# Four convolution layers on one core: the weights' preparation reordered, the interval layer's right products on two row tiles, roots by Newton steps, and fewer transfers for the images' parts

## The chip, the cores and the metric

One core of one Trainium2 chip runs the whole program. The metric is the device time of one execution in microseconds (us); it is compared as a median over several executions.

## What is computed

The input `x` is 4 images of 32 x 32 pixels with 16 channels, all fp32. Four layers follow, each with a group norm before it and a residual sum around it:

```python
x = x + conv(_gn(x), L0_M, L0_W, L0_G)
x = x + conv(_gn(x), L1_M, L1_W, L1_G)
x = x + interval(_gn(x), W0, b0, W1, b1, W2, b2)
x = x + conv(_gn(x), L3_M, L3_Wp, L3_G)
```

`_gn` subtracts a mean and divides by `sqrt(var + 1e-5)`, over all pixels and pairs of channels. In `conv`, each of the 1024 output positions has a 3 x 3 kernel of its own, from 16 to 16 channels:

```python
first   = einsum('ijyx,byxc->bijc', M, inputs)
shifted = conv2d(inputs, kernels of all (i, j, f))       # b, i, j, y, x, f
diff    = relu(inputs[:, None, None] - shifted)
second  = einsum('ijyx,bijyxc->bijc', W, diff)
return first - second
```

The interval layer takes running maxima and minima over a 32 x 32 table of each channel, and then two steps of `max_k sigmoid(f[i, k] Wf + r[k, j] Wr + b)` and a last product with a sigmoid.

## The kernel before

The images are worked on in two groups of two (`g` = 0, 1). A **phase** is one group in one of the three convolution layers; there are six, in the order (0,0), (1,0), (0,1), (1,1), (0,2), (1,2) of (group, layer). A phase has 8 chunks of 128 output positions, a chunk 32 **steps**, one for each of 16 channels `f` and 2 images `b`. So the program has 1536 steps, numbered here from 0. A step makes a 128 x 1024 sum in one of four pairs of PSUM banks: output positions on partitions, input pixels along the row, the left half of the image in one bank and the right half in the other.

**A step.** `first_part` (L642) issues eight fp32r matmuls with `ib` and `ia`, then ScalarE scales the sum in place (L663). `second_part` (L666), issued one step later, adds six matmuls with `iyz` and `im9`; then VectorE takes the minimum with zero, multiplies by the row of weights `WT` and sums (L680, output `junk`). Every product runs as two matmuls of 64 rows, on the upper and lower half of TensorE's rows. The 16 steps of the first two units (`u < PLAIN`) use plain fp32 products instead.

**Weights.** A unit `u` is four channels, eight steps; it is used in steps 8u to 8u + 7. `prep_parts` (L220) is a generator that is advanced once a step, from step `FIRST` = 3 on, and twice in steps 20 and 24. Its cycle has eight positions for each unit: the upper bits of the weights by VectorE (`upper`, L203); a masked copy `W9` by ScalarE (`halve`, L175); a scaled and a plain copy by ScalarE (L236, L240); differences, sums and four quarter copies by GpSimd (L237, L238, L241, L243, L245); `prep` of the next unit by GpSimd (L214); and at the seventh position two transfers on SyncE's queue that exchange halves of partitions of `parts` (L251), followed by the load of the raw weights of the unit after next (L110). Each `yield` names what other work may be done at that position: `IDLE`, `CALM`, both or none.

**Other work.** The generator `behind(phase)` (L733) prepares the next phase during this one and is advanced by `conv_layer` (L707) after the matmuls of a step have been issued. A positive number that it yields is a number of steps to wait; `IDLE` and `CALM` wait for a position of the weights' cycle that allows it. In it, `group_norm` (L312) makes mean and variance by VectorE and GpSimd and the root by ScalarE (L353, L358), with a reciprocal by VectorE (L360). `before_conv` (L368) transposes the normed images (L375), writes them to DRAM by eight transfers (`xs`, L381) and reads 24 shifted copies back (`raw`, L392), two a step, in layer 2 four a step. Then `split` (L274) takes upper and lower parts of an image (L203, L280, L284), `place` (L290) puts them into `ia` and `ib` by twelve transfers (L298, L300), `difference` (L286) makes `iyz` on GpSimd (L288), and `halve` and `halve_rest` (L178) make `im9`. `first_terms` (L418) makes the einsum with `M`: 128 matmuls on TensorE. `interval_layer` (L484) works on tables by VectorE scans (L527), GpSimd copies and selections (L534, L538) and products on TensorE: `left` (L544) and `right_side` (L555). The latter makes three blocks of 352, 231 and 110 columns one after the other, a step apart, each in a bank pair of its own, and ScalarE copies each to `rt` (L564).

**Order.** All is under `manual_schedule`: every engine and SyncE's queue works in the order in which the program issues, and waits in that order for what each instruction needs. Within a step the order is: the weights' generator, the first part, the second part of the step before, then `behind`.

Of the kernel before, what the change touches and what calls it, by code (L numbers as in the profile page):

```python
# [44 lines left out]
def net_kernel(ctx: ExitStack, tc: tile.TileContext, x, xq, xi, convs, iv_w, iv_b, out):  # L45
# [40 lines left out]
    def bank(name):  # L86
        return bank_pair(name)[:, 0]
# [131 lines left out]

    def prep_parts():  # L220
# [3 lines left out]

        for u in range(PLAIN, n_chunks * NU):
# [20 lines left out]
            yield ()  # L246
            prep(u + 1)
            yield (IDLE,)
            yield (IDLE, CALM)
            for h in range(2):  # L250
                nc.sync.dma_start(  # L251
                    parts[64 * h : 64 * h + 64, 1].bitcast(F32),
                    parts[64 - 64 * h : 128 - 64 * h, 0].bitcast(F32),
                )
            load_raw(u + RAWS)
            yield (IDLE, CALM)
            yield (IDLE, CALM)
# [12 lines left out]
    def halves(temp, b):  # L270
        v = temp.rearrange("p (k s b n) -> p k s b n", k=2, s=2, b=GB)
        return v[:, 0, :, b], v[:, 1, :, b]
# [17 lines left out]
    def place(g, b, temp):  # L290

        ty, tz = (v.bitcast(F32) for v in halves(temp, b))
        da, db = (v[g].bitcast(F32)[:, :, b] for v in (ia, ib))
        for h, (lo, hi) in enumerate(QUARTERS):
            for s in range(2):
                at = HW if s == h else 0
                for to, src in ((lo, ty), (hi, tz)):
                    nc.sync.dma_start(da[to, s, :LAST], src[lo, s, at : at + LAST])  # L298
            for to, src in ((lo, ty), (hi, tz)):
                nc.sync.dma_start(db[to], src[hi])  # L300
        yield 1
# [7 lines left out]
    def pair_view(ap):  # L309
        return ap.rearrange("p t (g s) -> p t g s", s=2)  # L310

    def group_norm(g, name, dst, gap):  # L312
# [55 lines left out]
    def before_conv(g, layer):  # L368
# [29 lines left out]
        temp = big.tile([P, 8192], F32R, tag="big", name=f"temp_{g}{layer}")[:, :TEMP]  # L398
# [19 lines left out]
    def first_terms(layer, mt):  # L418
# [3 lines left out]
        for g in range(NG):  # L422
            for pt in range(NT):
                for j in range(4):
# [4 lines left out]
                    )  # L429
        ft = work.tile([P, NG, NT * GC], F32, tag="fs", name=f"ft_{layer}")  # L430
# [15 lines left out]
    def constants():  # L446
# [7 lines left out]
        nc.gpsimd.tensor_scalar_mul(mask2[GC : 2 * GC], mask2[GC : 2 * GC], -1.0)  # L454
# [23 lines left out]
        for k, name in ((1, "r0"), (4, "r1")):  # L478
            t = const.tile([64, NQ * GB, C], F32, name=name)
# [4 lines left out]
    def interval_layer(g):  # L484
# [56 lines left out]
        )  # L541
        yield 5
# [12 lines left out]
        def right_side(name, wr):  # L555

            for k0 in range(0, T1, 11):
                j0 = k0 + 1
                ps = bank(f"ps_{name}{g}{k0}")
                n = T1 - j0  # L560
                nc.tensor.matmul(  # L561
                    ps[:, : 11 * n], lhsT=wr, rhs=r[:R, k0 : k0 + 11, j0:], start=True, stop=True
                )
                nc.scalar.copy(  # L564
                    rt[:, j0:, k0 : k0 + 11],
                    ps[:, : 11 * n].rearrange("p (k j) -> p j k", j=n),
                )
                yield 1
# [411 lines left out]
```

## Time and profile before

| what | us |
|---|---|
| median of three runs | 2478.37 (2478.10 to 2479.17) |
| the profiled execution | 2478.41 |
| its span, first to last instruction | 2476.7 |
| TensorE matmuls busy | 2458.2 |
| VectorE busy | 2087.3 |
| ScalarE busy | 1878.4 |
| GpSimd busy | 1579.7 |
| L680, VectorE, 1536 times | 1879.5 |
| L663, ScalarE, 1520 times | 1532.0 |
| five table loads on ScalarE, 1.283 each | 6.4 |
| landing of the exchange of halves, median | 4.9 |

The profile is of one execution; its own time of 2478.41 us has 1.7 us around the span. Busy shares are of the span. In lines of the timeline the first number is the start and the second the length, in us from the span's start; "x4" after the shape is the number of instructions merged into the line, and the bracket names what ended the idle time before it. `PE` is TensorE's matmuls, `PEld` its loads of stationary weights, `DVE` VectorE, `ACT` ScalarE, `POOL` GpSimd, and `SPq` the issuing of transfers by SyncE.

### The profile page before, as it was taken

Reading aid. Unit: us, or ns where it says so; the run is one execution under the profiler, and the core shown is the slowest. Engines: PE = TensorE matmul, PEld = TensorE weight load, DVE = VectorE, ACT = ScalarE, POOL = GpSimd, SP = SyncE. Lnnn points to the kernel's source line nnn. Section 1 sums busy time; section 2 is a strip of 40 time slices with the busy share of each in tenths; the row PEclk is TensorE's granted clock in tenths of the full one; section 3 lists DMA queues with packets and bytes.
Section 4 is the critical chain, followed back from the end, with each engine's and each line's share of the span. In section 5 each row is a group of like instructions: output and inputs, shape, how many; then the busy total and the mean of one; then the engine's idle time right before and its main releaser. Section 6 shows DMA issues by size and latency. Waiting matters only on the chain.

```text
span 2476.7 us, 58058 instructions
## 1 busy us (share of the span) xinstructions
PE 2458.2 (99%) x21906; PEld 2090.1 (84%) x21906; DVE 2087.3 (84%) x3617; ACT 1878.4 (76%) x2181; POOL 1579.7 (64%) x1750
## 2 busy tenths in 40 slices
PE   8999999999999999999999999999999999999999
PEld 5999888888888888888888988888998888888887
DVE  9888878888888888778898988899889888788887
ACT  4778767787777778777777777787777787677776
POOL 4766655666565657555567777586878676555552
PEclk9999999999999999999999999999999999999999
DMA  6446754466454467644454545574455467554442
GB/s 198 138 137 182 203 155 135 124 182 164 133 143 135 135 168 198 186 116 134 136 145 127 142 124 140 146 196 125 126 138 144 127 181 195 154 148 137 137 137 54
DMA packets 97673, 366.92 MB, mean 148 GB/s; under 512 B 26480, under 2 KB 31472, under 8 KB 97392
## 3 DMA queue, kind: packets, MB, share of 16 engines
q1 hardware_dynamic: 96832, 362.79, 53.0%
q8 instruction: 172, 2.82, 0.5%
q14 instruction: 109, 0.89, 0.1%
q10 hardware_dynamic: 432, 0.39, 0.1%
q0 software_dynamic: 128, 0.02, 0.0%
HBM read 199.78 MB, written 1.02 MB: 81 GB/s over the span
## 4 chain that ended last, share of the span: by engine, by line
PE 94%; DVE 2%; issue 1%; DMA 1%; ACT 0%; SPq 0%; POOL 0%; ACTq 0%; DVEq 0%; POOLq 0%
PE pc L627 93%; DVE junk L680 1%; PE pf L425 1%; DMA raw<-in_g 1%; ACT pc L663 0%; DMA first<-in_g 0%; SPq L298 0%; DVE raw L846 0%; SPq L300 0%; PE ps_l L548 0%; PE ps_r L561 0%; DMA parts<-parts 0%; DVE tables L508 0%; DVE raw L854 0%; DMA ib<-first 0%
## 5 line engine op out<-in xcount | busy, mean ns | idle before, releaser
L680 DVE SCALAR_TENSOR_TENSOR junk<-pc,WT 128x1024 f32<-128x1024 f32 x1536 | 1879.5, 1224 | 359.1 <-PE pc L627 308.3
L663 ACT ACTIVATE pc<-pc 128x1024 f32<-128x1024 f32 x1520 | 1532.0, 1008 | 561.0 <-PE pc L627 535.8
L627 PE MATMUL pc<-ib,parts 64*128 64x512 f32 x6080 | 958.5, 388 | 4.1 <-DVE junk L680 3.4
L627 PE MATMUL pc<-iyz,parts 64*128 64x512 f32 x6080 | 955.5, 387 | 2.2 <-ACT pc L663 2.0
L627 PE MATMUL pc<-ia,parts 64*128 64x496 f32 x6080 | 933.5, 379 | 0.0
L627 PEld LDWEIGHTS pc<-ia,parts 64*128 64x128 f32 x6080 | 595.5, 184 | 100.8
L627 PEld LDWEIGHTS pc<-ib,parts 64*128 64x128 f32 x6080 | 591.5, 184 | 105.0 <-DVE junk L680 9.9
L627 PEld LDWEIGHTS pc<-iyz,parts 64*128 64x128 f32 x6080 | 592.5, 184 | 88.4 <-ACT pc L663 6.4
L627 PE MATMUL pc<-im,W 64*128 64x496 f32 x3072 | 611.5, 384 | 0.0
L237 POOL TENSOR_TENSOR parts<-raw,upper_w 128x512 fp32r<-128x512 f32 x190 | 248.5, 1308 | 500.2 <-DVE upper_w L203 434.8
L627 PEld LDWEIGHTS pc<-im,W 64*128 64x128 f32 x3072 | 303.0, 184 | 54.5 <-issue 3.2
L243 POOL CAST parts<-parts 32x512 fp32r<-32x512 f32 x380 | 231.1, 608 | 50.1 <-ACT parts L240 31.8
L238 POOL TENSOR_TENSOR W<-W,raw 128x512 fp32r<-128x512 f32 x190 | 247.6, 1303 | 1.8 <-ACT W L175 1.8
L241 POOL TENSOR_TENSOR parts<-parts 128x512 fp32r<-128x512 f32 x190 | 246.8, 1299 | 2.0 <-ACT parts L236 1.9
L245 POOL CAST parts<-upper_w 32x512 fp32r<-32x512 f32 x380 | 231.6, 609 | 22.8
L214 POOL TENSOR_TENSOR raw<-raw,ident 128x512 f32<-128x512 f32 x190 | 199.9, 1052 | 52.2 <-DMA raw<-in_g 28.7
L175 ACT ACTIVATE W<-raw,low_w 128x512 fp32r<-128x512 f32 x190 | 136.2, 717 | 0.1
L680 DVE DVE_READ_ACCUMULATOR junk<-pc,WT 128x1 f32 x1536 | 127.5, 83 | 0.0
L236 ACT ACTIVATE parts<-upper_w 128x512 fp32r<-128x512 f32 x190 | 118.8, 625 | 6.6 <-DVE upper_w L203 6.4
L240 ACT CAST parts<-upper_w 128x512 fp32r<-128x512 f32 x190 | 116.5, 613 | 0.0
L695 POOL TENSOR_SCALAR acc<-acc 128x32 f32<-128x32 f32 x40 | 16.4, 409 | 141.7 <-DVE junk L680 139.7
L203 DVE TENSOR_SCALAR upper_w<-raw 128x512 int32<-128x512 int32 x190 | 86.1, 453 | 1.2 <-POOL raw L214 0.9
(139 smaller groups left out, 479.4 us busy)
## 6 DMA issues: line engine op xcount, KB each, us to landing
raw<-in_g SPq DMA_DIRECT2D x190, 768.0 KB, 7.1
parts<-parts SPq DMA_DIRECT2D x380, 384.0 KB, 4.9
WT<-in_w SPq DMA_DIRECT2D x48, 512.0 KB, 4.6
MT<-in_mt SPq DMA_DIRECT2D x24, 512.0 KB, 7.4
raw<-xs SPq DMA_DIRECT2D x120, 71.8 KB, 2.9
ib<-temp SPq DMA_DIRECT2D x40, 128.0 KB, 2.6
ia<-temp SPq DMA_DIRECT2D x80, 62.0 KB, 3.4
ib<-first SPq DMA_DIRECT2D x8, 128.0 KB, 2.4
```

What stands on the lines that cost most here:

```text
L175: nc.scalar.activation(dst, src, AF.Copy, scale=mask[:, 1:2])
L214: eng.tensor_tensor(raws[u][:, s, at:to], raws[u][:, s, at:to], pick[s][:, f0 + at : f0 + to].unsqueeze(2).to_broadcast([P, to - at, P]), ...
L236: nc.scalar.activation(WD, high, AF.Copy, scale=-EPS)
L237: nc.gpsimd.tensor_tensor(WL, w8, high, ALU.subtract)
L238: nc.gpsimd.tensor_tensor(W9, W9.bitcast(F32), src[:, 2], ALU.add)
L240: nc.scalar.copy(WU, high)
L241: nc.gpsimd.tensor_tensor(WD, WD.bitcast(F32), WL.bitcast(F32), ALU.add)
L243: nc.gpsimd.tensor_copy(WU[hi], WL[lo].bitcast(F32))
L245: nc.gpsimd.tensor_copy(WL[lo], high[hi])
L627: nc.tensor.matmul(ps[:, h, at : at + n], lhsT=w[r], rhs=v[r] if n == NH else v[r][:, :n], start=first and k == 0, stop=k == len(pairs) - ...
L663: nc.scalar.activation(ps, ps, AF.Copy, scale=1.0 + EPS)
L680: nc.vector.scalar_tensor_tensor(junk, ps.rearrange("p h n -> p (h n)"), 0.0, chunks[n], op0=ALU.min, op1=ALU.mult, accum_out=accs[phase][ ...
```

## The change

1. **The weights' cycle.** The masked copy `W9` comes first and the upper bits second, into a tile `high` of their own. The sum for `W9` and `prep` of the next unit come one operation group earlier, the quarter copies later, and the next load moves from the seventh position to the fifth. The exchange of halves moves to the second position of the next unit's cycle. The two extra advances are in steps 17 and 20.
2. **Right products.** The table `r` is copied to partitions 64 to 127 and the weights `r0`, `r1` are made for 128 partitions. The block of 352 columns runs on the first row tile, the blocks of 231 and 110 columns on the second, all issued together into one pair of banks. ScalarE's three copies are still a step apart.
3. **Roots.** The group norms' root and reciprocal are replaced by `inverse_root`: a start value from the bits of the number, by VectorE, and four Newton steps of four GpSimd operations each, spread over steps. The activation that loaded the Sqrt table ahead goes, and so does the one for the Sigmoid table in each interval step; a Sigmoid activation stands once in the first terms of layer 0.
4. **Images' parts.** `place` uses eight transfers instead of twelve: the four of `ib` first, then four of `ia`, each with two slots.
5. **Order of steps.** In the first chunk of each phase, not only of the first, the steps of each unit take image 0 first and then image 1.
6. `squares` uses the scratch tile `junk`, and `temp` is passed whole and cut in `halves`.

```diff
+    def exchange(parts):
+        if parts is not None:
+            for h in range(2):
+                nc.sync.dma_start(
+                    parts[64 * h : 64 * h + 64, 1].bitcast(F32),
+                    parts[64 - 64 * h : 128 - 64 * h, 0].bitcast(F32),
+                )
+
     def prep_parts():
+        swapped = None
         for u in range(PLAIN, n_chunks * NU):
...
-            high = upper(src[:, 0:1], 1, f"w{u}")[:, 0]
-            yield (IDLE,)
             halve(W9, src[:, 1], low_w)
             yield ()
+            high = work.tile([P, FU * P], F32, tag="high", bufs=2, name=f"high_{u}")
+            nc.vector.tensor_scalar(
+                high.bitcast(I32), w8.bitcast(I32), HIGH, None, op0=ALU.bitwise_and
+            )
+            exchange(swapped)
+            yield (IDLE,)
             nc.scalar.activation(WD, high, AF.Copy, scale=-EPS)
             nc.gpsimd.tensor_tensor(WL, w8, high, ALU.subtract)
-            nc.gpsimd.tensor_tensor(W9, W9.bitcast(F32), src[:, 2], ALU.add)
             yield ()
             nc.scalar.copy(WU, high)
+            nc.gpsimd.tensor_tensor(W9, W9.bitcast(F32), src[:, 2], ALU.add)
+            prep(u + 1)
+            yield ()
             nc.gpsimd.tensor_tensor(WD, WD.bitcast(F32), WL.bitcast(F32), ALU.add)
             for lo, hi in QUARTERS:
                 nc.gpsimd.tensor_copy(WU[hi], WL[lo].bitcast(F32))
             for lo, hi in QUARTERS:
                 nc.gpsimd.tensor_copy(WL[lo], high[hi])
-            yield ()
-            prep(u + 1)
+            load_raw(u + RAWS)
+            swapped = parts
             yield (IDLE,)
-            yield (IDLE, CALM)
-            for h in range(2):
-                nc.sync.dma_start(
-                    parts[64 * h : 64 * h + 64, 1].bitcast(F32),
-                    parts[64 - 64 * h : 128 - 64 * h, 0].bitcast(F32),
-                )
-            load_raw(u + RAWS)
-            yield (IDLE, CALM)
-            yield (IDLE, CALM)
+            for _ in range(3):
+                yield (IDLE, CALM)
+        yield (IDLE, CALM)
+        exchange(swapped)
...
     def place(g, b, temp):
...
+        for lo, hi in QUARTERS:
+            for to, src in zip((lo, hi), parts):
+                nc.sync.dma_start(db[to], src[hi])
         for h, (lo, hi) in enumerate(QUARTERS):
-            for s in range(2):
-                at = HW if s == h else 0
-                for to, src in ((lo, ty), (hi, tz)):
-                    nc.sync.dma_start(da[to, s, :LAST], src[lo, s, at : at + LAST])
-            for to, src in ((lo, ty), (hi, tz)):
-                nc.sync.dma_start(db[to], src[hi])
+            for k, to in enumerate((lo, hi)):
+                at = (2 * k * GB + b) * NH + HW * (1 - h)
+                pitch = GB * NH + HW * (2 * h - 1)
+                src = temp.bitcast(F32)[lo, at : at + 2 * pitch].rearrange("p (s n) -> p s n", s=2)
+                nc.sync.dma_start(da[to, :, :LAST], src[:, :, :LAST])
...
+    def inverse_root(v, name):
...
+        nc.gpsimd.tensor_scalar(a, v, 1.0 / (2 * NP), 1e-5, op0=ALU.mult, op1=ALU.add)
+        nc.vector.tensor_scalar(
+            t.bitcast(I32), a.bitcast(I32), 1, None, op0=ALU.logical_shift_right
+        )
+        nc.vector.tensor_scalar(
+            y.bitcast(I32), t.bitcast(I32), -1.0, float(0x5F3759DF), op0=ALU.mult, op1=ALU.add
+        )
+        nc.gpsimd.tensor_scalar_mul(a, a, -0.5)
+        for pause in (1, 1, IDLE, 2):
+            yield pause
+            nc.gpsimd.tensor_tensor(t, a, y, ALU.mult)
+            nc.gpsimd.tensor_tensor(t, t, y, ALU.mult)
+            nc.gpsimd.tensor_scalar(t, t, 1.5, None, op0=ALU.add)
+            nc.gpsimd.tensor_tensor(y, y, t, ALU.mult)
+        return y
...
-        nc.scalar.activation(spare, spare, AF.Sqrt)
         v = yield from totals(f"v{name}")
-        yield 2
-        yield IDLE
-        rstd = work.tile([P, GC // 2], F32, tag="rstd", name=f"rstd_{name}")
-        nc.scalar.activation(rstd, v, AF.Sqrt, bias=eps, scale=1.0 / (2 * NP))
-        yield 2
-        nc.vector.reciprocal(rstd, rstd)
+        rstd = yield from inverse_root(v, name)
...
+        if layer == 0:
+            nc.scalar.activation(spare, spare, AF.Sigmoid)
...
+        below = tables[R:, : T1 * T1].rearrange("p (i j) -> p i j", j=T1)
+        nc.gpsimd.tensor_copy(below, r[:R])
+        tops = (r[:R], below)
         yield 5
...
-            for k0 in range(0, T1, 11):
+            ps = bank_pair(f"ps_{name}{g}")
+            blocks = []
+            for k0, h, at in ((0, 0, 0), (11, 1, 0), (22, 1, 11 * (T1 - 12))):
                 j0 = k0 + 1
-                ps = bank(f"ps_{name}{g}{k0}")
                 n = T1 - j0
+                blocks.append((k0, j0, n, ps[:, h, at : at + 11 * n]))
                 nc.tensor.matmul(
-                    ps[:, : 11 * n], lhsT=wr, rhs=r[:R, k0 : k0 + 11, j0:], start=True, stop=True
+                    blocks[-1][3], lhsT=wr[R * h : R * h + R], rhs=tops[h][:, k0 : k0 + 11, j0:],
+                    start=True, stop=True,
                 )
+            for k0, j0, n, sums in blocks:
                 nc.scalar.copy(
...
-            nc.scalar.activation(spare, spare, AF.Sigmoid)
             yield 2
...
-            if n == 0:
+            if t == 0:
                 steps.sort(key=lambda s: (s[0] // FU, s[1]))
...
-                if n == 0 and at in (20, 24):
+                if n == 0 and at in (17, 20):
                     next(parts)
```

More of the change, by code (lines that the diff above doesn't have):

```diff
@@ L270, in halves @@
     def halves(temp, b):
-        v = temp.rearrange("p (k s b n) -> p k s b n", k=2, s=2, b=GB)
+        v = temp[:, :TEMP].rearrange("p (k s b n) -> p k s b n", k=2, s=2, b=GB)
         return v[:, 0, :, b], v[:, 1, :, b]
@@ L290, in place @@
     def place(g, b, temp):
-        ty, tz = (v.bitcast(F32) for v in halves(temp, b))
+        parts = halves(temp.bitcast(F32)[:, :TEMP], b)
         da, db = (v[g].bitcast(F32)[:, :, b] for v in (ia, ib))
+        for lo, hi in QUARTERS:
+            for to, src in zip((lo, hi), parts):
+                nc.sync.dma_start(db[to], src[hi])
         for h, (lo, hi) in enumerate(QUARTERS):
-            for s in range(2):
-                at = HW if s == h else 0
-                for to, src in ((lo, ty), (hi, tz)):
-                    nc.sync.dma_start(da[to, s, :LAST], src[lo, s, at : at + LAST])
-            for to, src in ((lo, ty), (hi, tz)):
-                nc.sync.dma_start(db[to], src[hi])
+            for k, to in enumerate((lo, hi)):
[3 more added lines that the diff above has]
+                nc.sync.dma_start(da[to, :, :LAST], src[:, :, :LAST])
         yield 1
@@ L310, in pair_view @@
         return ap.rearrange("p t (g s) -> p t g s", s=2)
+    def inverse_root(v, name):
+        n = GC // 2
+        a, y, t = (
+            work.tile([P, n], F32, tag=tag, name=f"{tag}_{name}") for tag in ("root_a", "root_y", "root_t")
+        )
[5 more added lines that the diff above has]
+            y.bitcast(I32), t.bitcast(I32), -1.0, float(0x5F3759DF), op0=ALU.mult, op1=ALU.add
+        )
+        nc.gpsimd.tensor_scalar_mul(a, a, -0.5)
[6 more added lines that the diff above has]
+        return y
     def group_norm(g, name, dst, gap):
@@ L397, in before_conv @@
         yield 6 if layer == 2 else 12
-        temp = big.tile([P, 8192], F32R, tag="big", name=f"temp_{g}{layer}")[:, :TEMP]
+        temp = big.tile([P, 8192], F32R, tag="big", name=f"temp_{g}{layer}")
         for b in range(GB):
@@ L452, in constants @@
         )
-        nc.gpsimd.tensor_scalar_mul(mask2[GC : 2 * GC], mask2[GC : 2 * GC], -1.0)
+        for at in (GC, 3 * GC):
+            nc.gpsimd.tensor_scalar_mul(mask2[at : at + GC], mask2[at : at + GC], -1.0)
         yield 2
@@ L478, in constants @@
         for k, name in ((1, "r0"), (4, "r1")):
-            t = const.tile([64, NQ * GB, C], F32, name=name)
+            t = const.tile([P, NQ * GB, C], F32, name=name)
             for q in range(NQ):
@@ L555, in right_side @@
         def right_side(name, wr):
-            for k0 in range(0, T1, 11):
+            ps = bank_pair(f"ps_{name}{g}")
+            blocks = []
+            for k0, h, at in ((0, 0, 0), (11, 1, 0), (22, 1, 11 * (T1 - 12))):
                 j0 = k0 + 1
-                ps = bank(f"ps_{name}{g}{k0}")
                 n = T1 - j0
+                blocks.append((k0, j0, n, ps[:, h, at : at + 11 * n]))
                 nc.tensor.matmul(
-                    ps[:, : 11 * n], lhsT=wr, rhs=r[:R, k0 : k0 + 11, j0:], start=True, stop=True
+                    blocks[-1][3], lhsT=wr[R * h : R * h + R], rhs=tops[h][:, k0 : k0 + 11, j0:],
+                    start=True, stop=True,
                 )
+            for k0, j0, n, sums in blocks:
                 nc.scalar.copy(
-                    rt[:, j0:, k0 : k0 + 11],
-                    ps[:, : 11 * n].rearrange("p (k j) -> p j k", j=n),
+                    rt[:, j0:, k0 : k0 + 11], sums.rearrange("p (k j) -> p j k", j=n)
                 )
@@ L821, in net_kernel @@
     s2 = const.tile([P, 1], F32, name="s2")
-    squares = const.tile([P, 256], F32, name="squares")
+    squares = work.tile([P, NP], F32, tag="junk", name="squares")[:, :256]
     nc.vector.scalar_tensor_tensor(
@@ L884, in rest_of_start @@
         yield 2
-        temp = first.bitcast(F32R)[:, used : used + TEMP]
+        temp = first.bitcast(F32R)[:, used:]
         for b in range(GB):
```

## The prediction

> **What bounds the kernel now.** I read the page's busy shares, then the chain that ended last, then TensorE's timeline wherever the chain leaves TensorE, then SyncE's queue beside it.
>
> ```profile
> PE 2458.2 (99%) x21906; PEld 2090.1 (84%) x21906; DVE 2087.3 (84%) x3617; ACT 1878.4 (76%) x2181; POOL 1579.7 (64%) x1750
> ...
> PE 94%; DVE 2%; issue 1%; DMA 1%; ACT 0%; SPq 0%; POOL 0%; ACTq 0%; DVEq 0%; POOLq 0%
> ```
> ```profile
> 535.28 401.52 PE pc L627 x3584
> ```
> The first shows TensorE busy for 99% of the span, the second (chain in order of time) an undisturbed stretch: 3584 matmuls are 256 steps of 14, so a step (one output channel of one image) takes 1.568 us. Nothing in the change makes a step shorter. What it can move are gaps: in the timeline I summed TensorE's waits over the usual 0.22 us between starts; from 43 us on they are 17.2 us in all, interval matmuls included. That caps any gain.
>
> SyncE's queue, in two stretches (start, duration, line, transfers):
> ```profile
> 34.16 1.19 SPq L251 DMA_DIRECT2D parts<-parts  x2
> 35.39 1.21 SPq L110 DMA_DIRECT2D raw<-in_g  x1
> 36.69 3.33 SPq L298 DMA_DIRECT2D ia<-first  x4
> 40.08 1.29 SPq L300 DMA_DIRECT2D ib<-first  x2
> 41.42 5.84 SPq L298 DMA_DIRECT2D ia<-first  x4
> 47.31 1.29 SPq L300 DMA_DIRECT2D ib<-first  x2
> ```
> ```profile
> 1581.78 5.26 SPq L381 DMA_DIRECT2D xs<-xt  x8
> 1587.82 5.70 SPq L392 DMA_DIRECT2D raw<-xs  x12
> 1593.68 1.11 SPq L251 DMA_DIRECT2D parts<-parts  x2
> 1594.84 1.36 SPq L110 DMA_DIRECT2D raw<-in_g  x1
> 1596.24 9.90 SPq L392 DMA_DIRECT2D raw<-xs  x12
> ```
> The reader is to see one queue worked off in program order, about 0.47 us a small raw transfer and 0.6 us others. A transfer also waits until the one eight places earlier has landed: of the last twelve, the eighth after the weights' load waits for the load (8.5 to 9.1 us from issue to landing here, 10.1 at 35.39). The exchange of halves (L251) lands 3.9 to 5.3 us after issue here, 3.7 to 6.3 at the start.
>
> **What the Trainium skill says.** ScalarE: Activation LUTs, "What ACT_TABLE_LOAD costs": 1283 ns and about 1380 ns of drain per switch of set. The trace has five loads of 1283 ns; what counts is TensorE's loss, below. SBUF — State Buffer, "Who interferes with whom": VectorE and GpSimd share a port pair as an exclusive lock, held for an instruction. The trace agrees: L203 on weights takes 0.42 us, but 1.07 at 2027.48, where GpSimd's L280 ran until 0.79 us after its start. TensorEngine Tiling (Array Packing), "Key Properties": tiles operate independently; here the two halves of a step start within 20 ns of each other, the fp32 steps of the start included.
>
> **Roots.** Four table loads (two at L591, two at L353) fall between steps.
> ```profile
> 1420.18 1.28 ACT L591 ACT_TABLE_LOAD   x1
> ...
> 1422.63 0.73 PE L627 MATMUL pc<-iyz,parts 64*128 64x512 f32 x4 [0.39 <-ACT pc L663]
> ```
> The matmul group before starts at 1421.64; 0.99 us later instead of 0.44 the next one, which runs 0.73 instead of 0.62: 0.66 us. 4 x 0.66 = **-2.65**. The Sigmoid load moves beside the 7.04 us of first terms, where ScalarE has nothing due (0; 0.66 if not covered). Added: 18 small GpSimd operations a norm, at 0.23 to 0.25 us (L459, L344) about 4.5 us, beside a unit's 7.5 us of 12.5: covered, but VectorE's two new operations wait for GpSimd's first in the middle of its queue. At the norms of phases 1 and 2 that is behind the copies, some 1.6 us, just within the two steps that PSUM's four bank pairs cover. In the two interval norms GpSimd's queue is 12.5 us for eight steps, so `xi` comes just in time: 0.3 each. Into VectorE's sum.
>
> **Right products.**
> ```profile
> 1327.97 0.75 PE L561 MATMUL ps_r<-tables,r 64*128 64x352 f32 x2
> 1328.57 0.74 PE L627 MATMUL pc<-ib,parts 64*128 64x512 f32 x4
> ...
> 1334.19 0.65 PE L548 MATMUL ps_l<-tables,f 64*32 64x264 f32 x8
> ```
> 0.60 us for the first block, and three steps to 1334.19 take 5.62 instead of 4.70: 1.52 a call. After: 352 columns on one half (0.60) beside 231 and 110 (0.40 + 0.19) on the other, 0.6. 4 x 0.92 = **-3.7** (bounds: -1.3 if the halves did not overlap, at 1.19 a call, to -4.0 if the restart is free too). GpSimd's new copy (1.3 us by L243's 0.61 for 512 elements) lies in five idle steps: 0.
>
> **The reordered cycle: where the exchange goes.** Unit u is used in steps 8u to 8u+7. Counting the yields, its cycle begins at step 8u-15; the exchange was at position 6, step 8u-9, ahead of that position's other work. Now it is at position 1 of the next unit's cycle, step 8u-6. In an empty queue that is harmless: GpSimd's copies end near 8u-8, and 5 us are 3.2 steps. But SyncE passes it in program order, so all that stands between the old and new place goes first; the second product of step 8u needs it.
> - *Layer 2's images (phases 3, 4).* Counting gives the transpose at step 978 before (the 12 raw transfers ahead of the exchange, as the trace has them) and 972 after. Then 8 `xs` transfers, a load (973), 16 raw transfers (974 to 977) and the exchange for step 984. On the clock of the first `xs` transfer (3.45 us after its step begins) 984's second product is due at 12 x 1.568 - 3.45 + 0.22 = 15.6. The queue: raw starts at 6.0, 16 x 0.475 = 7.6, so 13.6 at least, up to 16.7 with the wait for the load. Landing 0.5 + 3.9 to 5.3 later: 18 to 22. Stall 2.4 to 6.4; I take 5.0, twice: **+10.0**.
> - *Phase 0's second group.* 12 raw transfers and a load precede the exchange of step 106, due at 112: reached at 16, landed at 21.2, due at 18.7: **+2.5** (0 to 3.5). Phases 1 and 2 have 6 ahead of it and land about in time: +0.3 each, **+0.6**.
> - *Start.* The exchange of unit 2 was issued at 34.16, ahead of the second image's parts; now it stands behind them (step 12 against 11). Eight transfers from 35.8, the second waiting for VectorE's L280 (done 37.33), the eighth for the load: 41.8 to 42.9, landing 47 to 48.6. Step 16 starts at 43.1 and needs it at 43.3: stall 3.7 to 5.3. The old stall for the second image's `ib` (0.86 at 49.5) goes. **+3.5** (-0.9 to +4.5).
> - *Images' parts.* Eight transfers for twelve: 4 x 0.63 us less per image on the queue. But in phases 0 to 4 the next exchange now stands behind them, and they wait for L280 on GpSimd, which I place at 5 to 6 steps after its own. Eight transfers, exchange and landing: 9.9 us, 6.3 steps; needed within 6 or so: 0 to 2.2 us each, ten places, **+3.5** (0 to 8).
>
> **VectorE and ScalarE.** VectorE's mask of weights moves one step later. It leaves GpSimd's L280 and L288, but meets the table's copy (L534, 2.2 us) after the first scans: it comes 1.3 us after the scan and waits 0.9, on a backlog already at the limit: +0.9 in each interval. It also stands directly after halve_rest (L178, 0.74, or 1.9 with the lock) instead of a junk apart. VectorE's stalls are 6.4 us now, by the gaps they end; I put them at 8.4: **+2.0** (-3 to +5, for both new collisions and vanished ones). ScalarE: a step leaves 0.56 us; where an idle position is followed by another operation, one step is late by 0.1 to 0.3: **+0.3**. First image first in each phase: 0, no phase start waits for an image; if its cover were gone it saves three steps of waiting. Scratch tiles: 0.
>
> **Sum**, on the profiled execution's 2478.41 (span 2476.7 and 1.7 around it; 0.04 above the median): -2.65 - 3.7 + 10.0 + 2.5 + 0.6 + 3.5 + 3.5 + 2.0 + 0.3 = +16.05, so **2494.5**.
>
> **Rivals.** *Exchange in time (faster).* One mechanism: SyncE reaches each exchange early enough, in layer 2 before 15.6 - 5.3 = 10.3 on that clock, at the start before 38. For it: nothing waits for halves now, and in most cycles the queue has been waiting for GpSimd, not the reverse. Against: 0.47 us a raw transfer is measured. Then -6.35 - 0.86 + 0.3 + 0.5: 2472. *Half of it.* The load lands early, exchanges land in 3.9 us: 2 each in layer 2, 2 at the start, VectorE as above: -6.35 + 6 + 2.3 = +2, 2480.4. *Pile-up.* Bounds above all together, GpSimd late as well: +27, 2505. That the two halves of TensorE don't overlap is a bound above, 2.4 less gain.
>
> **Chances.** Forecast (2486 to 2504) 0.64, in time 0.14, half 0.14, pile-up 0.08. About 0.2%, 5 us, is what a measurement of this kernel can tell from no change. Faster 0.14 (in time); same 0.12 (most of half); slower 0.74. For 8 in 10 the range runs from 2474 to 2505, leaving out most of the faster case and of the pile-up.
>
> **What would show it.** In the waits, TensorE or its weight loads behind DMA parts<-parts near 43, 1590 and 2005 us, several us each, with SyncE's exchange after 16 raw transfers; two table loads instead of five; ps_r matmuls in one group of 0.6 us a call. Without the waits for parts, the steps on the exchange are wrong and the faster rival holds.

## The result, and the profile after

The changed kernel takes **2542.64 us** (median of five, 2536.98 to 2547.77); the kernel before takes 2478.37 us. The ratio is 1.0256, with a 95% interval of 1.0239 to 1.0273; by the medians it is 64 us slower. The direction was as forecast, the size was four times the +16 of the forecast and outside its range. The profiled execution took 2542.92 us, with a span of 2540.9.

On the page, the busy line and the chain:

```profile
PE 2481.8 (98%) x21906; PEld 2101.8 (83%) x21906; DVE 2091.9 (82%) x3625; ACT 1872.6 (74%) x2159; POOL 1603.1 (63%) x1897
...
PE 18%; DMA 0%; DVE 0%; ACT 0%; issue 0%; SPq 0%; DVEq 0%; ACTq 0%
```

TensorE has the same 21906 matmuls, and a pair still starts every 0.226 us. What grew is time between them. The chain explains only the last 18% of the span here, so I went on with the waits. Added up as in the prediction (what intervals between TensorE's starts have over the usual one, from 43 us on, intervals over 0.25 us only), they are 78.3 us for the 17.2 of before: 61 of the 64 us. With each interval put down to what ended it (an interval is longer than the idle time in the rows below), some 25 of the 61 are waits for the exchange of halves, 28 are waits for ScalarE (33 for 5 before), and 7 have no wait at all: there the matmuls run at half rate (below).

From the waits of the changed kernel (waiting engine and line, what ended the wait, us in total, times, longest):

```profile
ACT parts L249 <- DVE high L244: 45.0, 43, 4.2
PEld pc L663 <- ACT pc L699: 41.3, 58, 2.5
PEld pc L663 <- DMA parts<-parts: 25.6, 14, 3.9
...
PE pc L663 <- ACT pc L699: 21.3, 25, 2.0
PE pc L663 <- DMA parts<-parts: 20.2, 12, 3.5
...
DVE root_t_c L331 <- POOL root_a_c L330: 6.2, 6, 2.4
```

Two causes stand in the rows of `PE` (matmuls; the rows of `PEld`, the weight loads ahead of them, overlap these). TensorE waits 20.2 us for the exchange of halves, which the prediction expected. It waits as long, 21.3 us, for ScalarE's scaling of the sum (L699), which the prediction did not expect: ScalarE itself waits 45.0 us for VectorE's mask of the weights (L244). In the kernel before, the same two rows were small, and there was none of TensorE for the exchange:

```profile
ACT parts L236 <- DVE upper_w L203: 6.4, 5, 2.8
...
PE pc L627 <- ACT pc L663: 2.0, 5, 0.4
```

**The exchange.** SyncE's queue of the changed kernel, at the start and at the first images of layer 2:

```profile
35.92 3.56 SPq L306 DMA_DIRECT2D ib<-first  x4
39.52 2.52 SPq L312 DMA_DIRECT2D ia<-first  x4
42.14 1.19 SPq L223 DMA_DIRECT2D parts<-parts  x2
```
```profile
1609.68 3.79 SPq L409 DMA_DIRECT2D xs<-xt  x8
1613.57 0.39 SPq L110 DMA_DIRECT2D raw<-in_g  x1
1614.77 10.21 SPq L420 DMA_DIRECT2D raw<-xs  x16
1625.14 1.10 SPq L223 DMA_DIRECT2D parts<-parts  x2
```

And TensorE at that second place:

```profile
1625.08 0.39 PE L663 MATMUL pc<-ib,parts 64*128 64x512 f32 x2
1628.94 0.79 PE L663 MATMUL pc<-ib,parts 64*128 64x512 f32 x1 [3.47 <-DMA parts<-parts]
1630.87 0.79 PE L663 MATMUL pc<-ib,parts 64*128 64x512 f32 x1 [1.14 <-DMA parts<-parts]
```

The queue is as the prediction counted it: at the start the exchange is reached at 42.14 (forecast 41.8 to 42.9); in layer 2, 16 raw transfers stand ahead of it, and it is issued 15.5 us after the first `xs` transfer (forecast 13.6 to 16.7). Its two transfers land 3.8 and 5.7 us after the first is issued. TensorE waits for each in turn; with the gaps between the matmuls just behind them that is 5.6 us.

**The mask.** The timeline at another place, VectorE, ScalarE and TensorE:

```profile
248.71 1.70 DVE L178 SCALAR_TENSOR_TENSOR im<-raw,low_x,im 128x512 fp32r<-128x512 f32 x1
250.33 1.51 DVE L244 TENSOR_SCALAR high<-raw 128x512 int32<-128x512 int32 x1
251.87 0.63 ACT L249 ACTIVATE parts<-high 128x512 fp32r<-128x512 f32 x1 [2.47 <-DVE high L244]
252.41 1.01 ACT L699 ACTIVATE pc<-pc 128x1024 f32<-128x1024 f32 x1
253.47 0.73 PE L663 MATMUL pc<-iyz,parts 64*128 64x512 f32 x4 [1.98 <-ACT pc L699]
```

VectorE is busy with `halve_rest`, and the mask that follows takes 1.51 us instead of 0.42, while GpSimd's L298 runs beside it. ScalarE's first reading of the mask, L249, was issued one step after the mask; it stands at the head of ScalarE's queue for 2.47 us. The scaling L699 stands behind it. TensorE had finished the first part of that sum by 249.9 us, and needs it scaled for its next second part, at 253.47. Most masks are not lengthened: the median of the 190 is 0.42 us and only 7 take over 1 us, for 43 waits, so the place of the mask counts for more than its length. The Trainium skill, SBUF — State Buffer, section "Who interferes with whom", has the port pair of VectorE and GpSimd as an exclusive lock, which fits the 1.51 us; no run here tests the lock itself.

**The roots and the right products.** There are two table loads, the second here, beside the first terms:

```profile
339.66 1.28 ACT L459 ACT_TABLE_LOAD   x1
340.95 0.20 ACT L459 ACTIVATE spare<-spare 1x1 f32<-1x1 f32 x1
```

The next activation follows 0.01 us after the load, so the 1380 ns of drain that the prediction quotes do not show here.

The right products of one call, and the products that follow three steps later:

```profile
1363.17 0.75 PE L597 MATMUL ps_r<-tables,r 64*128 64x352 f32 x4
1363.50 0.66 PE L663 MATMUL pc<-ib,parts 64*128 64x512 f32 x1
1363.58 0.36 PE L597 MATMUL ps_r<-tables,r 64*128 64x110 f32 x2
...
1368.72 0.65 PE L582 MATMUL ps_l<-tables,f 64*32 64x264 f32 x8
```

They run beside each other in one group: the block of 110 columns starts at 1363.58, before the 0.75 us of the first line are over. From the first to `ps_l` it is 5.55 us for the 6.22 of the same call before.

### The profile page after: what moved, and what is told of

Read it like the earlier page. It is cut to its first block, busy times and chain, and to the rows that moved or that the text cites. A ratio compares the mean times of both kernels' runs of the same rounds, so it can differ in the third digit from the quotient of the medians.

```text
span 2540.9 us, 57954 instructions
## 1 busy us (share of the span) xinstructions
PE 2481.8 (98%) x21906; PEld 2101.8 (83%) x21906; DVE 2091.9 (82%) x3625; ACT 1872.6 (74%) x2159; POOL 1603.1 (63%) x1897
## 5 line engine op out<-in xcount | busy, mean ns | idle before, releaser
L699 ACT ACTIVATE pc<-pc 128x1024 f32<-128x1024 f32 x1520 | 1532.1, 1008 | 588.8 <-PE pc L663 569.8
L663 PE MATMUL pc<-ib,parts 64*128 64x512 f32 x6080 | 976.0, 389 | 25.2 <-DMA parts<-parts 20.2
L663 PE MATMUL pc<-iyz,parts 64*128 64x512 f32 x6080 | 973.1, 390 | 21.6 <-ACT pc L699 21.3
L663 PE MATMUL pc<-ia,parts 64*128 64x496 f32 x6080 | 948.8, 381 | 0.0
L663 PEld LDWEIGHTS pc<-ib,parts 64*128 64x128 f32 x6080 | 606.3, 185 | 128.5 <-DMA parts<-parts 25.6
L663 PEld LDWEIGHTS pc<-ia,parts 64*128 64x128 f32 x6080 | 608.4, 185 | 98.9
L250 POOL TENSOR_TENSOR parts<-raw,high 128x512 fp32r<-128x512 f32 x190 | 246.8, 1299 | 664.1 <-PE pc L663 537.5
L260 POOL CAST parts<-high 32x512 fp32r<-32x512 f32 x380 | 233.7, 615 | 22.8
L214 POOL TENSOR_TENSOR raw<-raw,ident 128x512 f32<-128x512 f32 x190 | 198.2, 1043 | 2.3 <-DMA raw<-in_g 2.3
L249 ACT ACTIVATE parts<-high 128x512 fp32r<-128x512 f32 x190 | 119.2, 627 | 48.8 <-DVE high L244 45.0
L252 ACT CAST parts<-high 128x512 fp32r<-128x512 f32 x190 | 116.0, 610 | 0.0
L244 DVE TENSOR_SCALAR high<-raw 128x512 int32<-128x512 int32 x190 | 91.5, 481 | 0.1
```

The source lines that it names most:

```text
L214: eng.tensor_tensor(raws[u][:, s, at:to], raws[u][:, s, at:to], pick[s][:, f0 + at : f0 + to].unsqueeze(2).to_broadcast([P, to - at, P]), ...
L260: nc.gpsimd.tensor_copy(WL[lo], high[hi])
L663: nc.tensor.matmul(ps[:, h, at : at + n], lhsT=w[r], rhs=v[r] if n == NH else v[r][:, :n], start=first and k == 0, stop=k == len(pairs) - ...
L699: nc.scalar.activation(ps, ps, AF.Copy, scale=1.0 + EPS)
```

## The experiments

Each run shares its chip with runs of the kernel before, and the ratios are to those. "Waits" is the sum defined above (before: 17.2 us).

### Exchange and mask, undone in the changed kernel

The first edit puts the exchange back where it was; the second moves the mask up beside the halving; the third run has both.

```diff
@@ first: prep_parts of the changed kernel
-            exchange(swapped)
             yield (IDLE,)
...
-            for _ in range(3):
-                yield (IDLE, CALM)
+            yield (IDLE, CALM)
+            exchange(parts)
+            yield (IDLE, CALM)
+            yield (IDLE, CALM)
@@ second
-            halve(W9, src[:, 1], low_w)
-            yield ()
             high = work.tile([P, FU * P], F32, tag="high", bufs=2, name=f"high_{u}")
             nc.vector.tensor_scalar(...)
+            halve(W9, src[:, 1], low_w)
+            yield ()
```

> The changed kernel, with the exchange of halves put back to its old place (eight steps and one before the unit's first use, before the next images' transfers in SyncE's queue); all else as changed. Theory E (the exchange is issued too late by SyncE, behind the images' transfers): TensorE's waits for parts go, some 23 us more than before, and with them the matmuls at half rate after four of these stalls, some 6 us: about 2542.6 - 28 = 2515 us. Rival to E (GpSimd's copies end late, so the place in the queue is immaterial): within 4 us of 2542. Rival to my second theory (ScalarE's waits are a consequence of the exchange): those waits, 27 us, go as well, and the time falls to about 2490.

**2522.75 us** (ratio 1.0177, 1.0161 to 1.0192): 20 us come back, not 28. Waits 59.2 us; TensorE's for the exchange fall only from 20.2 to 10.3 (matmul row), and those for ScalarE stay:

```profile
ACT parts L247 <- DVE high L243: 42.6, 43, 4.7
...
PE pc L660 <- ACT pc L696: 18.5, 25, 2.0
...
PE pc L660 <- DMA parts<-parts: 10.3, 5, 3.3
```

So ScalarE's waits are no consequence of the exchange, and the old place removes only half of the exchange's waits. The rest is at layer 2's images, where the exchange stands behind raw transfers at its old place too:

```profile
1598.63 14.04 SPq L417 DMA_DIRECT2D raw<-xs  x20
...
1613.31 1.11 SPq L223 DMA_DIRECT2D parts<-parts  x2
```

In this run and in the changed kernel, layer 2's first `xs` transfer is issued after 973 of VectorE's evictions, in the kernel before after 979. The images' steps come six steps earlier, as the prediction had counted.

> The changed kernel, with VectorE's mask of the weights (high) one position earlier, beside the halving of W9, so that two steps and not one lie between it and ScalarE's first reading of it; all else as changed. Theory H (ScalarE stands in its queue behind a late mask, and the scaling that TensorE needs stands behind it): TensorE's waits for ScalarE's scaling fall from 26 to some 4 us, with 1.6 us of half rate: about 2542.6 - 24 = 2518 us. Rival (VectorE is late whatever the place of the mask, and TensorE then waits for VectorE's evictions instead): 2535 to 2545 us, with waits for junk in place of those for ScalarE.

**2523.36 us** (1.0177, 1.0162 to 1.0192): 19 us come back. Theory H holds in its rows:

```profile
PE pc L663 <- DMA parts<-parts: 22.7, 19, 3.0
...
PEld pc L663 <- ACT pc L699: 4.8, 14, 0.8
...
ACT parts L249 <- DVE high L242: 4.7, 4, 2.1
```

One position takes the mask's waits from 45.0 to 4.7 us, with the same operations. The waits for the exchange rise a little, from 20.2 to 22.7 us.

> The changed kernel with both edits, exchange at its old place and mask one position earlier. If theories E and H are both right and add up: 2542.6 - 28 - 24 = about 2490 us, what is left being VectorE's waits for the Newton roots and the late tables, some 6 us, and the start, less the gains of right products and roots. If the two are one disturbance: not below 2505 us.

**2495.17 us** (1.0062, 1.0047 to 1.0077), waits 35.2. The two are worth 47.5 us together: by the medians 8 us more than the sum of the single ones, by the profiled executions only 2 us more, so whether they hide each other is not shown. 17 us remain.

### Each alone in the kernel before

```diff
@@ fourth
-            high = upper(src[:, 0:1], 1, f"w{u}")[:, 0]
             yield (IDLE,)
             halve(W9, src[:, 1], low_w)
+            high = upper(src[:, 0:1], 1, f"w{u}")[:, 0]
             yield ()
@@ fifth: the exchange of unit u - 1 beside the halving of unit u
             halve(W9, src[:, 1], low_w)
+            exchange(swapped)
             yield ()
```

> The kernel before, with the mask of the weights one position later only, so that one step lies between it and ScalarE's first reading. Theory H: the mechanism needs nothing else of the change: 20 to 25 us more, about 2500 us, with ScalarE's waits for the mask at some 40 us. Rival (it takes the reordered GpSimd work or the Newton roots to make the mask late): 2478 to 2483 us.

**2508.90 us** (1.0121, 1.0104 to 1.0138): 31 us, more than expected, from one instruction a unit that is moved by one step.

```profile
PEld pc L627 <- ACT pc L663: 42.0, 56, 2.1
ACT parts L236 <- DVE upper_w L203: 40.0, 41, 4.8
PE pc L627 <- ACT pc L663: 20.8, 29, 1.7
```

This is the mechanism without any other part of the change. It could have been read from the trace of before: for each of the 190 units I took the time from the end of the mask to ScalarE's first reading. Its median is 1.75 us, but in 71 units it is less than a step of 1.568 us; what these lack adds up to 42.7 us. The 45.0 us of ScalarE's waits in the changed kernel and the 40.0 here are near that sum. The kernel loses less than ScalarE waits: 31 us here, for 40.0.

> The kernel before, with the exchange of halves three steps later only (beside the next unit's halving, six steps before use). Theory E: the place in SyncE's queue is enough to cost what the forecast put on it and what its undoing gave back, 20 us: about 2498 us, with TensorE's waits for parts in phase 0's second group, before layer 2's images and at the start. Rival (the exchange is late only together with the images' steps that the Newton roots move): 2480 to 2486 us.

**2529.04 us** (1.0196, 1.0182 to 1.0211): 50 us, far more than the 20 expected. TensorE waits for the exchange 32.5 us (matmul row, 19 times; 40 us by the intervals between starts), and 11 us of matmuls at half rate come on top (below). Beside the places of the forecast there are now waits behind the images' parts, for instance about 1.5 us each at 254 and 268 us. So theory E's mechanism holds, and the rival falls. That the changed kernel's earlier load and shorter `place` soften it there, where the exchange costs some 30 us, was not tested.

### The other parts, alone

> The kernel before, with the right products on two row tiles only (and GpSimd's copy of the table that they need). The forecast's term: -3.7, 2474.5 us. The trace of the changed kernel has its four calls with their next two steps at about 5.55 us for the 6.22 of before: -0.67 a call, -2.7: 2475.5 us. Rival (GpSimd's copy, 1.3 us, delays the weights' work and VectorE after it): 2478 us or more.

2477.24 us, ratio 0.9994 (0.9986 to 1.0002): a gain of 1.5 us by the ratio that the interval doesn't separate from none. Its trace has the four calls at 5.57 to 5.68 us for 6.08 to 6.23: -2.1 us together. Neither GpSimd's copy nor a missing overlap shows.

> The kernel before, with the Newton roots only (and the Sigmoid table loaded once). The forecast's terms: -2.65 for four table loads, and less than 1 us of VectorE's waits: 2476 us. Theory N (VectorE stands behind GpSimd's first operation at each norm, and the interval tables start late, 3.8 us by TensorE's waits in the changed kernel at the tables and 1.7 at two norms): about 2478.2 - 2.65 + 5.5 = 2481 us. A third possibility: the norm's other pauses move the images' transfers against the exchange, as the run with both edits shows behind 20 raw transfers, 7 us in each of layer 2's two images: 2490 us or more.

2487.15 us, ratio 1.0027 (1.0016 to 1.0038): **+6.7 us** by the ratio, 7.9 by the medians, where the forecast had -2. The queue of VectorE and GpSimd at one norm of layer 2:

```profile
1578.66 0.22 POOL L328 TENSOR_TENSOR root_t_c<-root_a_c,root_y_c 128x16 f32<-128x16 f32 x1
...
1579.60 0.22 POOL L331 TENSOR_TENSOR root_y_c<-root_y_c,root_t_c 128x16 f32<-128x16 f32 x1
1579.78 1.04 POOL L214 TENSOR_TENSOR raw<-raw,ident 128x512 f32<-128x512 f32 x1
1580.86 0.43 DVE L203 TENSOR_SCALAR upper_w<-raw 128x512 int32<-128x512 int32 x1 [2.00 <-POOL raw L214]
...
1582.48 0.74 PE L644 MATMUL pc<-ib,parts 64*128 64x512 f32 x4 [0.67 <-DVE junk L697]
```

Four of the small operations stand ahead of the weights' subtraction L214, which the mask L203 waits for; VectorE's evictions stand behind the mask. VectorE's waits for L214 rise from 0.9 to 8.6 us, those for GpSimd's first root operation from none to 3.2; TensorE's matmuls wait for VectorE's evictions 8.8 us, for 3.4 before.

> Everything of the change but the weights' cycle: Newton roots, right products on two row tiles, images' parts by eight transfers, first image first. Theory E with H (all of the loss is in the cycle): between 2472 and 2481 us. Rival (a part of the loss, the exchange behind the images' transfers in layer 2 that the run with both edits still shows, comes with the roots' pauses or the transfers, not with the cycle): 2485 to 2495 us.

2496.31 us, ratio 1.0070 (1.0057 to 1.0084): the rival holds. 7 us are the roots; the rest is in two places of layer 2 where VectorE stands up to 3.8 us for GpSimd, which stood behind the images' transfers. That led to the next runs.

> The kernel before, with the images' parts by eight transfers instead of twelve only. Forecast: nothing lost by itself, the queue is free some 2.5 us earlier per image: 2476 to 2480 us. Theory S (in the run of all but the cycle, GpSimd's subtraction for the second image stood behind the first image's ia transfers, VectorE's mask behind GpSimd, TensorE behind VectorE, 7 us at each image of layer 2; the eight transfers make that wait, since each now reaches over the second image's part of the same tile): about 2490 us, with that wait of GpSimd in layer 2.

2488.77 us, ratio 1.0039 (1.0025 to 1.0052): +9.7. What follows on what at one of the two places, in the order of time:

```profile
2042.44 1.21 POOL L280 TENSOR_TENSOR temp<-raw,upper_x 128x512 fp32r<-128x512 f32 x1 [4.68 <-DMA ia<-temp]
...
2047.66 1.04 POOL L214 TENSOR_TENSOR raw<-raw,ident 128x512 f32<-128x512 f32 x1
...
2048.73 1.41 DVE L203 TENSOR_SCALAR upper_w<-raw 128x512 int32<-128x512 int32 x1 [5.41 <-POOL raw L214]
...
2051.34 1.22 PE L629 MATMUL pc<-ib,parts 64*128 64x512 f32 x4 [4.78 <-DVE junk L682]
```

> The kernel before, with the first image's steps first in every phase's first tile only (not only in the first phase). Forecast's term: 0, 2476 to 2481 us. Rival (the order moves the steps at which the second image's parts are needed, or the accumulations that GpSimd waits for, and with theory S out it is this that the run of all but the cycle shows in layer 2): about 2490 us.

2478.34 us, ratio 0.9998 (0.9990 to 1.0006): nothing, as forecast.

> The changed kernel with exchange and mask early as in the third run, and with the roots by ScalarE's table and VectorE's reciprocal as in the kernel before. Theory N (the Newton roots cost 7 us net, as alone in the kernel before): 2495.2 - 7 = 2488 us. Theory R (they also moved the images' transfers against the exchange, which costs the two waits of 5.5 us and their 2.3 us at half rate in layer 2): 2495.2 - 7 - 15 = 2473 us.

2492.29 us (1.0054, 1.0039 to 1.0068): 3 us for the 7 of theory N, and theory R falls; the two waits in layer 2 are still there (4.4 us at 2018), so the roots' pauses are not what moved the images. The runs with the old cycle, the seventh and eighth among them, all have 979 evictions ahead of layer 2's first `xs` transfer, and this one has 973: the move comes with the cycle.

> The kernel before with the right products on two row tiles, and with Newton roots on VectorE alone: three rounds of three operations, fused, in the pauses of before, no table loads but two. If the roots' loss was GpSimd's (the weights' subtraction behind 18 small operations, VectorE's mask behind that): 2479 - 2.65 - 2.1 + 0 to 1 = 2474 to 2475.5 us. Rival (twelve more small operations on VectorE, 2 us a norm, bring its stalls): 2479 us or more.

```diff
-        nc.scalar.activation(rstd, v, AF.Sqrt, bias=eps, scale=1.0 / (2 * NP))
-        yield 2
-        nc.vector.reciprocal(rstd, rstd)
...
+        for pause in (2, IDLE, 2):
+            yield pause
+            nc.vector.scalar_tensor_tensor(t, a, -0.5, rstd, op0=ALU.mult, op1=ALU.mult)
+            nc.vector.tensor_tensor(t, t, rstd, ALU.mult)
+            nc.vector.scalar_tensor_tensor(rstd, t, 1.5, rstd, op0=ALU.add, op1=ALU.mult)
```

2483.51 us, ratio 1.0018 (1.0010 to 1.0025), with the gain of the right products in it: the rival. VectorE's own stalls eat more than the table loads gave (TensorE's matmuls wait 9.4 us for it; 3.4 before).

### The two causes that were open

The thirteenth run lays the scratch tile out image by image and keeps the eight transfers; the fourteenth adds the right products. The edit is shown against the ninth run.

```diff
-        v = temp[:, :TEMP].rearrange("p (k s b n) -> p k s b n", k=2, s=2, b=GB)
-        return v[:, 0, :, b], v[:, 1, :, b]
+        v = temp[:, :TEMP].rearrange("p (k b s n) -> p k b s n", k=2, s=2, b=GB)
+        return v[:, 0, b], v[:, 1, b]
...
-                at = (2 * k * GB + b) * NH + HW * (1 - h)
-                pitch = GB * NH + HW * (2 * h - 1)
+                at = 2 * (k * GB + b) * NH + HW * (1 - h)
+                pitch = NH + HW * (2 * h - 1)
```

> The kernel before with eight transfers per image, and with the scratch tile laid out image by image, so that no transfer's range reaches over the other image's part. Theory S (range overlap makes GpSimd's subtraction for the second image wait for the first image's ia transfers): the two waits of layer 2 go, 2477 to 2480 us. Rival (ib ahead of ia in the queue, or the longer transfers, make the loss): 2486 us or more, as with the overlap.

2477.15 us, ratio 0.9992 (0.9984 to 1.0001). The 10 us are gone, waits 17.6, and no wait of GpSimd for `ia<-temp` is left. With the same transfers in the same order, the overlap of ranges was the cause: a transfer with two slots reaches, from its first to its last element, over the other image's part, and the write there was made to wait for it. Whether the chip or the program's own ordering makes it wait, no run shows.

> As the run before this, with the right products on two row tiles besides. Theory S and the right products' 2.1 us by their trace: 2475 to 2477.5 us, the fastest so far if so. Rival to S: 2484 us or more.

**2476.30 us**, ratio 0.9986 (0.9980 to 0.9993): 3.4 us faster than the kernel before, small, but the interval excludes none. It is the fastest version here by its median; its interval overlaps those of the sixth and thirteenth runs.

The next two move layer 2's transpose and what follows six steps later in the third run's kernel, to where they were before; the sixteenth has the scratch tile image by image too, and the last one changes the roots as well.

```diff
         yield from group_norm(g, f"c{g}{layer}", xn, 1 if layer == 2 else 4)
+        if layer == 2:
+            yield 6
```

> The changed kernel with exchange and mask early, as in the third run, and the images' steps of layer 2 from the transpose on six steps later, where they were before. Theory E widened (the exchange waits behind raw transfers wherever these come ahead of it in the program): the two waits of 5.5 us and 2.3 us of half rate in layer 2 go, 2495.2 - 15 = 2480 us, if the later parts are not late themselves. Rival (GpSimd's copies, one position later than before, make the exchange late): within 4 us of 2495.

2487.93 us (1.0038, 1.0025 to 1.0052), 7 us less, half of what was expected. No matmul at half rate is left, and TensorE's waits for the exchange fall from 9.9 to 3.6 us (matmul rows). The place of the images' transfers in the program was a part of it. Another part of what remains is at the start, where TensorE waits for GpSimd's quarter copies, which the new cycle issues one position later:

```profile
45.48 0.82 PE L662 MATMUL pc<-ib,parts 64*128 64x512 f32 x4 [2.59 <-POOL parts L256]
```

> As the run before this, with the scratch tile laid out image by image. Theory S adds little here (2 us of GpSimd's waits for ia transfers in the third run): 2477 to 2482 us if theory E widened holds. Rival: more than 5 us below the run before this, then the overlap costs here too.

2488.46 us (1.0031, 1.0019 to 1.0043), not the 2477 to 2482 expected: no change; with this cycle the overlap cost nothing, as GpSimd's waits had it.

> As the sixteenth run (exchange and mask early, images six steps later, scratch tile image by image), with the roots by ScalarE's table and VectorE's reciprocal as in the kernel before. If the rest is the Newton roots: 2488.5 - 6.7 = 2481.8 us, with VectorE's waits at the interval's tables as before, 0.4 us each and not 2.6 in two. Rival (the rest is the exchange of phase 0 and the start, or GpSimd's copies one position later): 2486 us or more.

2484.95 us (1.0024, 1.0011 to 1.0037): between the two. The waits at the interval's tables fall to 0.36 us each, as expected, but four table loads are back, and so is a wait of 3.5 us for the exchange at the first images of layer 2, with 2.6 us more lost at half rate. The wait for GpSimd's copies at the start is there too, 2.1 us. How the last 6 us divide was not tried further.

## Why the prediction was wrong

The direction rests on the exchange, whose mechanism was forecast; the size does not. Even with the mask early the kernel takes 2523.36 us, above the range. By the prediction's own terms, with what was measured in their place:

| term | forecast | measured |
|---|---|---|
| exchange: layer 2, phase 0, phases 1 and 2, start, images' parts | +20.1 | 30.3 in the trace, half rate included; 20 to 28 by undoing its place |
| ScalarE | +0.3 | +19 to +28 |
| VectorE | +2.0 (0.6 of it at the roots) | +2.0 by TensorE's matmul rows (3.4 to 5.4), +0.3 by the intervals |
| roots | -2.65, with VectorE's 0.6 | +6.7 (alone, in the kernel before) |
| right products | -3.7 | -1.5 (-2.1 by its trace) |
| first image first | 0 | 0 |

- **The step that failed is ScalarE's.** The prediction wrote: "a step leaves 0.56 us; where an idle position is followed by another operation, one step is late by 0.1 to 0.3: +0.3". It counted ScalarE's time and took its operands as ready. In the part on VectorE it noticed that the mask moves a step later, and asked only what VectorE would collide with, not who reads the mask, and when: the distance to ScalarE's first reading fell from two steps to one. Undoing that distance alone gives 19 us, after the exchange is undone 28, and making it alone costs 31.
- **The exchange was right in mechanism and, place by place, too small.** That undoing its place alone gives back 20 us, the forecast's sum, is chance: half of the waits remained in that run. From the trace, each place less what it had before: start 3.5 us (forecast 3.5), layer 2 13.7 (10.0), phase 0 5.5 (2.5), phases 1 and 2 7.0 (0.6), images' parts 0.6 (3.5). Three sizes were off. Each exchange is two transfers that TensorE waits for in turn, the second 1.8 to 1.9 us after the first in the stalls that begin at 43, 200 and 1625 us, and the stall was priced by one: in phase 0 the exchange was issued 16.9 us after the first `xs` transfer (forecast 16) and landed at 20.8 (forecast 21.2) and at 22.7. In phases 1 and 2 six raw transfers stood ahead of it as counted, but its second transfer landed 7.6 and 5.7 us after the first was issued, not 3.9 to 5.3, and in phase 2 the next exchange stood behind ten more and was waited for as well (1.37 us at 946). And after some of these stalls TensorE ran at half rate, which the prediction did not have.
- **Half rate.** The clock and busy times in three stretches around the stall of phase 0, and in one at the start (stretch, its length, busy us and instructions of TensorE, its weight loads, VectorE, ScalarE and GpSimd, then granted clock, DMA share and GB/s):

```profile
200.00:204.50 4.50, 1.14 (x9) 0.41 (x5) 1.34 (x4) 0.72 (x1) 1.37 (x3) 1.00 0.92 211
204.50:209.00 4.50, 4.50 (x26) 3.74 (x28) 1.23 (x2) 2.36 (x3) 0.00 (x0) 0.62 0.91 263
209.00:213.00 4.00, 4.00 (x39) 3.60 (x38) 3.33 (x6) 3.12 (x5) 1.88 (x2) 1.00 1.06 240
...
48.20:51.60 3.40, 3.40 (x19) 3.29 (x19) 0.00 (x0) 1.73 (x2) 0.15 (x1) 0.50 0.86 237
```

  After 3.8 us of waiting (nine matmuls in 4.5 us) the clock is 0.62 and 26 matmuls fill the next 4.5 us, where 39 fit into 4.0 later; pairs start every 0.41 to 0.43 us, for 0.226. The Trainium skill, TensorE: Matmul & The Clock Gate, section "Part 1: The HAM clock gate (the "warmup" mystery)", says that the array falls to half its clock after an idle window of about 3.4 us, that this window runs free of the program, and that 512 columns then start 426.7 ns apart. The trace agrees in the rate. It differs in the stall that is enough: 2.2 us at one place and 2.7 at another, shorter than that window. It happens in six places of the changed kernel: in five of them it costs 1.2 to 1.8 us each, 7.3 us in all; the sixth is the last line, where the two halves of a pair start 0.1 us and more apart, not within 20 ns as the prediction read it, so that the sum of waits misses most of the loss: some 1.3 us, an estimate from 19 matmuls at 0.226 us a pair. In the kernel before, no matmul after 43 us runs so.
- **Roots: wrong in sign.** The four table loads went as forecast: in the seventh run what TensorE loses to ScalarE falls from 5.1 to 2.6 us. The prediction placed the 18 GpSimd operations "beside a unit's 7.5 us of 12.5: covered". That is the mean; in the queue four of them stand ahead of the weights' subtraction, and the mask on VectorE behind that. In the changed kernel `xi` came 1.9 us late and VectorE's transposes stood for it; TensorE then stood 2.2 us in two waits at each interval, for 0.4 before; the forecast had 0.3 more.
- **Right products: right, half the size.** The group takes about 0.9 us with what the steps beside it lose, not 0.60: 5.55 to 5.68 us for three steps of 4.70.
- **Images' parts.** The prediction looked at the queue. What decided is which bytes a transfer spans: 10 us in the kernel before. In the changed one GpSimd's waits for `ia<-temp` are 1.0 us in all; why they are so short there was not tested.

Summed along one path: 2542.64, less 19.9 (exchange back), less 27.6 (mask up), less 7.2 (images six steps later) is 2487.93; what is left, 9 us, is near the roots' 6.7 with the wait for GpSimd's copies at the start (2.6) and for the exchange in phase 0 (TensorE's 2.6 us at 196 us) and less the right products' 2. That last division is argued from the parts, and the seventeenth run does not confirm it in full. The prediction's rivals all turned on the exchange, the pile-up on GpSimd as well; none had ScalarE.

## What to carry to other kernels

When an operation is moved in a hand-ordered program, measure in the trace of before the time from its end to the start of each of its readers, for every instance and not as a mean, and subtract the move: what falls below zero is the wait to come, and it is paid by everything queued behind the reader. Do the same for a transfer in a shared queue, with every transfer that it now stands behind, and with half rate added when TensorE will stand for some two microseconds or more. When transfers are merged, look at the range that the merged one spans, because writes into its gaps may wait for it, as they did here.

## What was not expected of the hardware

- A stall of TensorE can cost again by two fifths or more: 3.8 us of waiting at 200 us were followed by 1.6 us lost at half rate. A stall of 2.2 us at 1341.64 was followed by it (four matmuls then took 1.03 us, and 1.6 us were lost), one of 2.1 us at 251.11 was not.

```profile
1344.08 0.73 PE L663 MATMUL pc<-iyz,parts 64*128 64x512 f32 x4 [2.04 <-ACT pc L699]
...
1345.35 1.03 PE L663 MATMUL pc<-ia,parts 64*128 64x496 f32 x4
```

  In the traces of all nineteen kernels, after 43 us, each of the 21 single stalls above 2.4 us was followed by half rate within 5 us, and 10 of the 21 stalls of 1.8 to 2.4 us were (some of these are one piece of a stall in two).

- Small operations on GpSimd cost by their place: 0.22 us each, but four ahead of a 1.04 us subtraction made VectorE stand 2.0 us.
- The exchange's two transfers land 3.8 and 5.7 us after the first is issued, with the raw transfers in flight; TensorE pays for the later one.
